# Graph attention with residual LayerNorm: the first edge of each query in blocks of its own, added by VectorE instead of TensorE

## The chip, the cores and the metric

The kernel runs on one core of a Trainium2 chip. The metric is the device time of one execution in microseconds (us). Each kernel was timed on one chip, with the kernel before run beside it in the same rounds. The series of experiments lie on different chips: e1 to e4, and later g1 and g2, on one, f1 to f4 on a second, h1 and h2 on a third. The kernel before took 2595.96 to 2599.37 us on them (medians), so a comparison across series, such as h1 with e2, is good to some 0.3%. All executions that are compared were in the fast state: those of one kernel agree within about half a per cent.

## The reference, cut to what matters

```python
# x: (16, 1024, 512), adj: (1024, 1024) of 0 and 1, the same for all 16 graphs
def _L0_gnn_ref(x, adj, Wq, bq, Wk, bk, Wv, bv, Wo, bo):
    B, N, D, H = (4, 2048, 512, 8); HD = D // H
    b, n, d = x.shape
    q = (x @ Wq + bq).reshape(b, n, H, HD)      # k and v alike
    scores = jnp.einsum('bqhd,bkhd->bhqk', q, k) / jnp.sqrt(jnp.float32(HD))
    scores = scores + (1.0 - adj)[None, None, :, :] * -1000000000.0
    attn = jax.nn.softmax(scores, axis=-1)
    out = jnp.einsum('bhqk,bkhd->bqhd', attn, v).reshape(b, n, d)
    return out @ Wo + bo

x = _layernorm(x + _L0_gnn_ref(x, adj, ...), axis=-1)
```

In these inputs all biases are zero. The adjacency is sparse, so the kernel works on edges and not on the full matrix of scores.

## The kernel before

One "batch" is one of the 16 graphs. Its 1024 queries are eight tiles of 128. The edges of a tile are packed into blocks of 128 edges, one edge to a partition. For each block GpSimd issues two gathers (the q row, and the k and v rows, of each edge). VectorE multiplies q by k and reduces to eight scores, ScalarE takes the exponentials, VectorE weighs v by them (`pv`), and TensorE adds the 128 weighed rows into their queries: a matmul with a matrix of zeros and ones, accumulated in PSUM over the blocks of a tile.

```python
BLOCKS = (11, 6, 4, 4, 3, 3, 3, 3)      # blocks of each tile: 37 a batch
...
def fill_psum(name):                     # all other outputs of TensorE
    return psum.tile([P, HALF], F32, tag="fill", name=name, bufs=4)
...
def add_up(n):
    b, t, i = blocks[n]
    if i == 0:
        SUM[b, t] = psum.tile([P, 2, HALF], F32, tag="sum", name=f"sum_{b}_{t}", bufs=2)
    ...                                                     # two matmuls into it
    if i == BLOCKS[t] - 1:
        later(1, lambda: normalise(b, t))                   # one block later
```

TensorE's other work (the products for q, k and v of the next batch, called "units" here, and the output products `po` of the finished tiles) fills the time between the sums. A loop over the blocks, run when the program is built, deals it out in equal shares, and so fixes the order on every engine:

```python
while n < total or plan or urgent or done or finishing:
    if front_batches < B and front_batches <= max(n // NB, 0) + 1:
        fronts += [...]                  # the next batch's units are let in at block 0
    ...
    elif n % NB == 0:                    # the share of one block, set once a batch
        tiles = len(done) + (NT if n + NB < total else NT + 2)
        share = (sum(u[0] for u in fronts) + tiles * NPAIR * PRODUCT) / NB
    weigh(n + 1); scores(n + 2)
    for fn in plan.pop(n, ()): fn()      # what was put off: normalise, y, ...
    exponentials(n + 2); add_up(n)
    credit += share
    while credit > 0 or urgent:
        ...                              # give out units while there is credit
    credit = min(credit, share)
    n += 1
```

An output tile is finished so: GpSimd adds a bias to the row of x that was loaded for it (`y`), VectorE adds the output product out of PSUM to `y` and takes the statistics, GpSimd makes the scale from them in three small instructions, and ScalarE applies it.

## Time and profile before

| | before |
|---|---|
| time, median of 3 | 2593.45 us (2592.3 to 2593.49) |
| TensorE (PE) busy | 2477.6 us |
| VectorE (DVE) busy | 1968.2 us |
| GpSimd (POOL) busy | 1499.0 us |
| ScalarE (ACT) busy | 698.7 us |
| a steady batch, mean of the fourteen between the first and the last | 153.6 us |

In this table and in those below a batch runs from VectorE's first reduction to scores in it to that in the next. The prediction counts from TensorE's first sum instead; this is why its first batch and last stretch are 147.1 and 135.6 us, and mine 148.9 and 140.3 us.

The busy column of PE is long because ends of matmuls are modelled. The measure that I use below is therefore made from starts: for each matmul the distance to the next start, less the median distance of its kind (0.429 us for a pass of a 512-wide product, 0.222 for a sum, 0.109 for a transpose), summed over a steady batch. I call this sum the **excess** of a batch. It holds both the idle time of TensorE and time at a lower pace, and is good to about 0.1 us. In the kernel before it is 3.16 us, of which 2.07 us are marked idle.

What matters most for this study is the change from one batch to the next. This is the timeline of TensorE there in the kernel before (start, length, instruction; in brackets the idle time before it and what ended it):

```profile
1073.85 0.67 PE L545 MATMUL sum<-pv,sums 128*128 128x256 f32 x2
...
1074.80 3.60 PE L377 MATMUL pq<-wq,xT 128*128 128x512 f32 x8
1078.23 2.74 PE L377 MATMUL pk<-wk,xT 128*128 128x512 f32 x6
1082.85 0.70 PE L545 MATMUL sum<-pv,sums 128*128 128x256 f32 x2 [1.88 <-DVE pv L533]
```

The sum at 1073.85 is block 0 of the new batch, the one at 1082.85 is block 1. Between them TensorE has seven products of the new batch to do, 6.0 us, and then stands for only 1.88 us, although VectorE takes 9.1 us from its weighing of block 0 (1073.02) to that of block 1 (1082.11).

### The profile page before, as it was taken

The numbers are of one execution on the slowest core, as the hardware profiler recorded it, in microseconds if no ns is written. First come the engines' busy times: TensorE is split into PE (matmuls) and PEld (weight loads), VectorE is DVE, ScalarE is ACT, GpSimd is POOL, SyncE is SP. The second block draws the span as 40 slices with busy tenths as digits, with TensorE's granted clock in tenths as the row PEclk, the third lists the DMA queues.
The fourth block names the chain that finished last, engine by engine and source line by source line (L and its number), as shares of the span: only waits on it lengthen the run. The fifth ranks groups of instructions, "written<-read, shape, count | busy, mean of one in ns | idle before, by whom it ended". The sixth has DMA issues, their size and how long they took to land.

```text
span 2594.1 us, 26742 instructions
## 1 busy us (share of the span) xinstructions
PE 2477.6 (96%) x7659; PEld 1352.6 (52%) x7659; DVE 1968.2 (76%) x3613; ACT 698.7 (27%) x1764; POOL 1499.0 (58%) x1717
## 2 busy tenths in 40 slices
PE   6988999999999999999999999999999999999967
PEld 3545555555555555555555555555555555555534
DVE  5668778778778877877777777877877777787766
ACT  1345322222222222222222222222222222222254
POOL 0156755647566574756647465564756557475675
PEclk9989999999999999999999999999999999999978
DMA  4368887887879788787878878787887978878785
GB/s 154 110 243 290 270 291 247 286 270 271 283 237 307 254 291 267 257 292 244 301 253 292 271 235 306 244 294 256 277 288 233 309 251 287 264 256 287 230 277 179
DMA packets 228679, 678.01 MB, mean 261 GB/s; under 512 B 29454, under 2 KB 29466, under 8 KB 228524
## 3 DMA queue, kind: packets, MB, share of 16 engines
q0 software_dynamic: 132608, 465.64, 56.3%
q1 hardware_dynamic: 93344, 205.60, 21.2%
q10 hardware_dynamic: 2572, 4.99, 0.5%
q8 instruction: 62, 1.02, 0.2%
q14 instruction: 93, 0.76, 0.1%
HBM read 541.86 MB, written 134.25 MB: 261 GB/s over the span
## 4 chain that ended last, share of the span: by engine, by line
PE 68%; POOL 11%; DVE 10%; issue 7%; ACT 2%; DMA 1%; ACTq 0%; POOLq 0%; another core or an unknown queue 0%; SPq 0%; DVEq 0%
PE pv L377 16%; PE pk L377 15%; PE pq L377 15%; PE sum L546 7%; PE sum L545 7%; POOL kvg L506 4%; PE po L377 4%; POOL y L461 3%; POOL qg L501 2%; DVE y L468 2%; DVE stats L471 2%; PE pxT L359 2%; PE poT L566 2%; DVE qg L515 1%; DVE pv L533 1%
## 5 line engine op out<-in xcount | busy, mean ns | idle before, releaser
L501 POOL DMA_INDIRECT qg<-q_rows,query_row x592 | 586.9, 991 | 588.1 <-DVE s L517 453.7
L506 POOL DMA_INDIRECT kvg<-kv_rows,key_row x592 | 588.7, 994 | 195.2 <-issue 182.9
L533 DVE TENSOR_TENSOR pv<-kvg,pv 128x512 f32<-128x512 f32 x550 | 394.3, 717 | 223.1 <-ACT pv L522 146.8
L377 PE MATMUL pq<-wq,xT 128*128 128x512 f32 x1024 | 482.7, 597 | 14.7 <-ACT xT L363 13.2
L377 PE MATMUL pk<-wk,xT 128*128 128x512 f32 x1024 | 488.9, 598 | 7.1 <-ACT xT L363 7.1
L377 PE MATMUL pv<-wv,xT 128*128 128x512 f32 x1024 | 479.1, 593 | 0.0
L377 PE MATMUL po<-wo,oT 128*128 128x512 f32 x1024 | 473.9, 602 | 0.0
L515 DVE TENSOR_TENSOR qg<-qg,kvg 128x512 f32<-128x512 f32 x592 | 432.6, 731 | 0.3 <-issue 0.3
L517 DVE TENSOR_REDUCE s<-qg 128x8 f32<-128x512 f32 x592 | 406.1, 686 | 20.5
L545 PE MATMUL sum<-pv,sums 128*128 128x256 f32 x1184 | 361.6, 387 | 46.4 <-DVE pv L533 33.8
L545 PEld LDWEIGHTS sum<-pv,sums 128*128 128x128 f32 x1184 | 222.2, 192 | 326.5 <-issue 239.0
L522 ACT ACTIVATE pv<-s 128x8 f32<-128x8 f32 x592 | 124.1, 210 | 929.2 <-DVE s L517 626.5
L546 PE MATMUL sum<-pv,sums 128*128 128x264 f32 x1184 | 366.6, 392 | 4.6 <-ACT pv L529 2.3
L377 PEld LDWEIGHTS pk<-wk,xT 128*128 128x128 f32 x1024 | 194.3, 192 | 193.3 <-issue 175.7
L377 PEld LDWEIGHTS po<-wo,oT 128*128 128x128 f32 x1024 | 192.9, 194 | 182.6 <-issue 173.3
L377 PEld LDWEIGHTS pv<-wv,xT 128*128 128x128 f32 x1024 | 190.5, 191 | 167.0 <-issue 158.4
L377 PEld LDWEIGHTS pq<-wq,xT 128*128 128x128 f32 x1024 | 187.1, 192 | 159.2 <-issue 135.0
L546 PEld LDWEIGHTS sum<-pv,sums 128*128 128x128 f32 x1184 | 226.2, 192 | 41.6 <-ACT pv L529 6.4
L461 POOL TENSOR_TENSOR y<-y,bo_bc 128x512 f32<-128x512 f32 x128 | 163.4, 1277 | 141.5 <-ACT pv L522 74.7
L468 DVE TENSOR_TENSOR y<-po,y 128x512 f32<-128x512 f32 x128 | 88.0, 688 | 151.5 <-POOL y L461 139.4
L404 DVE TENSOR_TENSOR kv<-pk,bk_bc 128x512 f32<-128x512 f32 x128 | 88.2, 689 | 115.8 <-PE pk L377 87.2
L389 DVE TENSOR_REDUCE nrm<-sq 128x8 f32<-128x512 f32 x256 | 172.9, 676 | 1.4 <-ACT sq L388 1.4
(98 smaller groups left out, 1664.8 us busy)
## 6 DMA issues: line engine op xcount, KB each, us to landing
kv_rows<-kv SPq DMA_DIRECT2D x128, 512.0 KB
x<-in_x_dram SPq DMA_DIRECT2D x128, 256.0 KB
q_rows<-q SPq DMA_DIRECT2D x128, 256.0 KB
y<-in_x_dram SPq DMA_DIRECT2D x128, 256.0 KB
out_dram<-y SPq DMA_DIRECT2D x128, 256.0 KB
qg<-q_rows,query_row POOLq DMA_INDIRECT x592
kvg<-kv_rows,key_row POOLq DMA_INDIRECT x592
a<-in_adj_dram SPq DMA_DIRECT2D x8, 512.0 KB
```

The lines of the kernel that those rows point to most:

```text
L377: nc.tensor.matmul(p, lhs()[:, ts(c, P)], w[:, c, :], start=(c == 0), stop=(c == NPAIR - 1))
L389: later(1, lambda: nc.vector.tensor_reduce(NRM[b][:, i, t, :], sq.rearrange("p (h d) -> p h d", d=HD), axis=AX.X, op=OP.add))
L461: later(2, lambda: nc.gpsimd.tensor_tensor(Y[b, t], Y[b, t], bo_bc, op=OP.add))
L468: nc.vector.tensor_tensor(y, p, y, op=OP.add)
L501: nc.gpsimd.indirect_dma_start(out=QG[n], out_offset=None, in_=q_rows[b % 2], in_offset=bass.IndirectOffsetOnAxis(ap=query_row[:, g:g + 1] ...
L506: nc.gpsimd.indirect_dma_start(out=KG[n], out_offset=None, in_=kv_rows[b % 2], in_offset=bass.IndirectOffsetOnAxis(ap=key_row[:, g:g + 1], ...
L515: nc.vector.tensor_tensor(m, m, KG[n][:, 0:D], op=OP.mult)
L517: nc.vector.tensor_reduce(S[n], m.rearrange("p (h d) -> p h d", d=HD), axis=AX.X, op=OP.add)
L522: nc.scalar.activation(PV[n][:, D:], S.pop(n), AF.Exp)
L533: nc.vector.tensor_tensor(pv[:, 0:D].rearrange("p (h d) -> p h d", d=HD), v[:, D:].rearrange("p (h d) -> p h d", d=HD), pv[:, D:, None].to ...
L545: nc.tensor.matmul(SUM[b, t][:, 0, 0:HD2], m, pv[:, 0:HD2], **kw)
L546: nc.tensor.matmul(SUM[b, t][:, 1, 0:HD2 + HEADS], m, pv[:, HD2:], **kw)
```

## The change

Each query's first edge goes into a block of its own per tile, with edge number p in partition p. Such a block needs no matrix to sort its rows, so VectorE can add it to the tile's sums directly. A batch still has 37 blocks, but TensorE sums only 29. The first-edge block is the last block of its tile. Its q rows are the tile's rows in order, so a plain load replaces the gather. The sums take one PSUM buffer instead of two, and the two banks that come free go to the other outputs, six instead of four.

```diff
-BLOCKS = (11, 6, 4, 4, 3, 3, 3, 3)
+BLOCKS = (10, 5, 3, 3, 2, 2, 2, 2)
+SUM = 0.87
...
-            return psum.tile([P, HALF], F32, tag="fill", name=name, bufs=4)
+            return psum.tile([P, HALF], F32, tag="fill", name=name, bufs=6)
... (the packing of edges leaves out each query's first one)
-                SUM[b, t] = psum.tile([P, 2, HALF], F32, tag="sum", name=f"sum_{b}_{t}", bufs=2)
+                PSUM[b, t] = psum.tile([P, 2, HALF], F32, tag="sum", name=f"sum_{b}_{t}", bufs=1)
...
-            if i == BLOCKS[t] - 1:
-                later(1, lambda: normalise(b, t))
...
+            nc.vector.tensor_tensor(r, s[:, 1, HD2:HD2 + HEADS], pv[:, D:], op=OP.add)
+            nc.vector.tensor_tensor(
+                o.rearrange("p (a d) -> p a d", a=2), s[:, :, 0:HD2], pv[:, 0:D].rearrange("p (a d) -> p a d", a=2),
+                op=OP.add,
+            )
             nc.vector.reciprocal(r, r)
... (one 512-wide product by r instead of two of half the width)
-                    share = (sum(u[0] for u in fronts) + tiles * NPAIR * PRODUCT) / NB
+                    share = (sum(u[0] for u in fronts) + tiles * NPAIR * PRODUCT + NS * SUM) / NB
...
+                if 0 <= n < total and blocks[n][2] == BLOCKS[blocks[n][1]]:
+                    normalise(n)
                 for fn in plan.pop(n, ()):
                     fn()
                 if 0 <= n + 2 < total:
                     exponentials(n + 2)
-                if 0 <= n < total:
+                credit += share
+                if 0 <= n < total and blocks[n][2] < BLOCKS[blocks[n][1]]:
                     add_up(n)
+                    credit -= SUM
...
-                credit += share
```

## The prediction

> **What bounds the kernel now.** I read the page's first two parts first: is one engine full, and for how much of the span?
>
> ```profile
> span 2594.1 us, 26742 instructions
> PE 2477.6 (96%) x7659; PEld 1352.6 (52%) x7659; DVE 1968.2 (76%) x3613; ACT 698.7 (27%) x1764; POOL 1499.0 (58%) x1717
> ...
> PE   6988999999999999999999999999999999999967
> ```
>
> TensorE is full from the second slice to the second last. VectorE is next with 76%. But a busy PE need not be a PE at its pace, so I read the order of time inside one block of edges (TensorE alone; start, length, instruction):
>
> ```profile
> 1001.64 0.59 PE L545 MATMUL sum<-pv,sums 128*128 128x256 f32 x2
> 1002.07 0.61 PE L546 MATMUL sum<-pv,sums 128*128 128x264 f32 x2
> 1002.52 3.60 PE L377 MATMUL pv<-wv,xT 128*128 128x512 f32 x8
> 1005.95 0.59 PE L545 MATMUL sum<-pv,sums 128*128 128x256 f32 x2
> ```
>
> No "idle before" mark stands anywhere. The cost of a thing is the distance between starts, not the length shown: one block's sum takes 1002.52 - 1001.64 = 0.88 us, and four 512-wide products (eight passes) take 1005.95 - 1002.52 = 3.43 us, 0.86 us each. Over the whole trace the median distances give 0.216 + 0.216 + 0.223 + 0.222 = 0.877 us for a block's sum. A batch of the steady part has 128 products, 37 sums, 16 groups of four transposes (0.44 us) and one mean (0.86 us): 109.8 + 32.4 + 7.0 + 0.9 = 150.1 us. Measured from the first sum of one batch to that of the next it takes 153.3 to 154.5 us, of which PE covers about 151.3. So over fourteen sixteenths of the kernel the time is PE's work plus some 2 us a batch. The waits of TensorE say where those are:
>
> ```profile
> PE sum L545 <- DVE pv L533: 33.8, 21, 2.4
> PE pq L377 <- ACT xT L363: 13.2, 1, 13.2
> PE poT L566 <- DVE o L557: 11.2, 13, 5.6
> ```
>
> The first is 1.9 us once at each change of batch: there PE has run out of units and VectorE is late. In time, VectorE alone:
>
> ```profile
> 1080.37 0.69 DVE L468 TENSOR_TENSOR y<-po,y 128x512 f32<-128x512 f32 x1 [5.34 <-POOL y L461]
> ...
> 1082.11 0.68 DVE L533 TENSOR_TENSOR pv<-kvg,pv 128x512 f32<-128x512 f32 x1
> ```
>
> While output tiles are finished, GpSimd's own round (two gathers of about 1.0 us, the add of 1.27 us, three small ones of 0.95 us together, gaps) repeats every 5.17 us, against 4.3 us of PE, and VectorE waits for it, so its lead of about 6.7 us (median from a block's weighing to its sum) is eaten by the end of the batch. The first batch has 19.8 us and the last stretch, 135.6 us from its first sum, has 42.0 us of PE idle: those two are not PE's.
>
> **What the Trainium skill says.** "Perfetto Trace Analysis", section "Tensor Engine Instruction (MATMUL, LD_WEIGHTS)": the end of a matmul in the trace is estimated from its size, not observed. This trace agrees: passes of 0.59 us start 0.43 us apart, so I cost by starts and not by the busy column (361.6 + 366.6 us over 592 blocks would give 1.23 us a block, 40% too much). "PSUM — Partial Sum Buffer", section "Specifications (TRN2)": eight banks of 2 KiB per partition. A sum tile takes two, so two of them and four fill banks before, one and six after, is all of it both times; the second sum buffer is really gone. "VectorE: DVE Perf Modes", section "The perf-mode tier table (the rule you actually need)": an fp32 tensor_tensor runs at 1x from SBUF or PSUM alike. The trace agrees: 688 ns for y<-po,y out of PSUM, a median of 684 ns for qg<-qg,kvg. "SBUF — State Buffer", section "Who interferes with whom": a VectorE instruction with two SBUF inputs contends with a GpSimd one that reads SBUF. The trace fits: that same product has a mean of 731 ns and a longest of 2156 ns.
>
> **The change, part by part.** *Blocks.* 37 blocks a batch become 29 summed ones and 8 of first edges; the gathers, scores, exponentials and weighings stay at 592. The capacity suffices: counted from the inputs, the fullest tile has 1276 edges beyond the first of each query, for 10 x 128 = 1280 places, so the slow fallback is not taken. *TensorE* loses 16 x 8 = 128 sums: 128 x 0.877 = 112.3 us. 120 of them lie in the first fifteen batches. In the thirteen steady ones and the second, 14 x 8 x 0.877 = 98.2 us, everything counts, since PE is the path there. In the first batch, where PE idles 19.8 of 147.1 us for VectorE and ScalarE, I count half of 7.0 us, 3.5 us. In the last stretch none for PE.
>
> *VectorE.* Before, a tile's end costs 0.157 + 0.203 us and two half products that take 0.76 us together: 1.12 us. After, an 8-wide add (estimate 0.16 us, from the 0.157 us of the like-sized row), a 512-wide add of PSUM and SBUF (0.69 us, from y<-po,y), the reciprocal 0.20 us, and a 512-wide product within SBUF (0.72 us, from pv<-kvg,pv): 1.77 us. That is +0.65 us x 128 = 83 us, 5.2 us a batch: 120 us of 153 become 125 of about 147, 85%. It lies beside PE's work. *GpSimd* loses 128 q gathers of 0.99 us (127 us); SyncE issues them as plain 256 KB loads, seven buffers ahead, as the gathers were. *DMA* moves the same bytes in less time: 261 GB/s becomes about 271. The DMA did not hold VectorE up (0.3 us of idle before all 592 products of q and k), so this is hidden.
>
> *Even steps.* The new share charges the sum to the credit, so a block of first edges gets about one more product. PE's time per step stays even, near 4.0 us.
>
> *The single buffer.* The first sum of a tile now waits until VectorE has added the last tile's sums. In VectorE's order these adds follow the next block's weighing (0.7 us), the scores of the one after (1.4 us) and their own 0.9 us: the sum can start some 2.3 us after the weighing it already waited for. Between the two sums lies the block of first edges, in which PE has about 4 us of other units. I laid this demand on the trace before, asking at each tile's first sum how long before it the next scores had ended, less 1.0 us: it holds by 1.2 to 6.1 us in 99 of 112 steady tiles, and fails by 2.2 us in the first tile of a batch, where PE has no units in between. There sum, adds and next sum form a chain; but VectorE is late there for GpSimd's sake, and what is waited for at the first sum is not waited for at the second (the 1.9 us above). Net I count 0 to 2 us a batch, 1 us, 15 us in all, less 3 us for the gathers that GpSimd no longer issues in that very round (three first-edge blocks among its last nine steps).
>
> *Last stretch.* Eight gathers fewer on GpSimd (8 us of its 88.5), 5 us more on VectorE (85.5), neither full: -2 us, and +0.6 us for the longer last tile.
>
> Sum: -98.2 - 3.5 + 15 - 3 - 2 + 0.6 = -91 us; 2593.5 - 91 = 2502. With six fill banks instead of four I expect nothing, since no listed wait of PE is for a free bank. I round to 2500.
>
> **The rivals.** (1) *The single buffer bites at every tile*: 2.3 us x 128 = 294 us if PE waited the full chain each time, or about 100 us if a third did. This would cancel the gain (2500 to 2700 us). For it: strict order on VectorE, which runs fuller than before. Against it: the leads of 1.2 to 6.1 us measured above, and that the adds stand where the old end of tile stood, for which VectorE hardly waited (1.1 us before rden). (2) *VectorE becomes the bound*: its own 125 us, with 8.7 us of waits for GpSimd's y and 9 us for exponentials a batch (139.4 and 146.8 us over 16), come to 143 us against PE's 147. Near, but part of the waits for exponentials is ScalarE standing behind PE's own outputs. If it came true, perhaps 149 to 151 us a batch: 2530 to 2560 us. (3) *The boundary gets better than I count*, since GpSimd's round shortens: no new waits at all, 2485 us. (4) *The loads of q queue up behind SyncE's waits* (508.4 us of it for y before a store): they have some 24 us of lead (six steps of 4.0), so I give it little; it would show as tens of us.
>
> **Range and chances.** The main term is exact work of the full engine; the doubt is all in how much of it new waits return. 2482 (rival 3) to 2530 (rival 2 at its mild end) should hold it 8 times in 10. Faster by over 2% means below 2541.6: 0.92. Within 2%: 0.07. Slower: 0.01.
>
> **What would show it.** PE's busy time should fall by somewhat more than 112 us (by its inflated column 128 x 1.23 = 157 us, to about 2320), with 928 passes per line of the sums where there were 1184; a steady batch should take 146 to 148 us; VectorE's busy time should rise by about 80 us to 2050; the wait of sum for VectorE's add should be about 15 times 1 to 3 us, at the changes of batch alone. I am wrong in the single-buffer step if that wait appears some 100 times, in the VectorE step if weighed blocks (pv) come late all through a batch, and in the main term if PE's gaps grow without either.

## The result

| | before, same rounds | after |
|---|---|---|
| time, median of 4 | 2593.47 us (2592.3 to 2597.06) | 2680.2 us (2679.08 to 2682.64) |
| ratio | 1 | 1.0333, 95% interval 1.0315 to 1.0351 |
| PE / DVE / POOL busy | 2477.6 / 1968.2 / 1499.0 us | 2386.0 / 2005.0 / 1395.7 us |
| first batch / steady batch / last stretch | 148.9 / 153.6 / 140.3 us | 144.4 / 159.7 / 147.2 us |
| excess of a steady batch | 3.16 us | 16.04 us |

A ratio here and below is the mean time of one kernel's fast runs over that of the kernel before in the same rounds, so it is not quite the ratio of the medians. The kernel became 3.3% slower, where I had predicted 3.6% faster. The page of the changed kernel, in its first two parts:

```profile
span 2680.9 us, 25437 instructions
...
PE 2386.0 (89%) x7123; PEld 1273.8 (48%) x7123; DVE 2005.0 (75%) x3637; ACT 695.5 (26%) x1764; POOL 1395.7 (52%) x1589
PE   7988798998989989798997989899898997989765
PEclk9989899998989989898998989999898998989877
```

TensorE did lose work: 536 matmuls (512 of them passes of the sums) and 91.6 us of its busy time. But its row of full slices now has an 8 or a 7 in every second or third place, and its granted clock (PEclk) dips in the same rhythm. Forty slices and sixteen batches: something happens once a batch. The waits of TensorE give it one name (total, times, longest):

```profile
PE sum L562 <- DVE rden L575: 230.2, 23, 15.3
```

230.2 us is more than twice the whole expected gain, and it is 23 waits, fifteen of them over 13 us (there are fifteen changes of batch), not the 128 that a wait at every tile would give. The timeline of TensorE at the change of batch, to be compared with the one of before above:

```profile
1093.03 0.59 PE L562 MATMUL sum<-pv,sums 128*128 128x256 f32 x2
1093.46 0.61 PE L563 MATMUL sum<-pv,sums 128*128 128x264 f32 x2
1107.80 1.19 PE L562 MATMUL sum<-pv,sums 128*128 128x256 f32 x2 [13.72 <-DVE rden L575]
1108.78 1.09 PE L563 MATMUL sum<-pv,sums 128*128 128x264 f32 x2
1109.66 1.91 PE L385 MATMUL pq<-wq,xT 128*128 128x512 f32 x2
```

The sum at 1093.03 is block 35, the last summed block of the old batch, and the one at 1107.80 is block 0 of the new batch. There is no product between them: TensorE has no product to do in blocks 35 and 36, and stands 13.72 us. The starts after it show a second loss: two sum passes take 0.98 us instead of 0.43, and one product takes 1.71 us (1109.66 to the next start at 1111.37) instead of 0.86. TensorE runs at half its pace for some 5 us after the stall, which costs another 2.5 us here. What VectorE does in these 14 us, in its own timeline:

```profile
1094.14 0.69 DVE L476 TENSOR_TENSOR y<-po,y 128x512 f32<-128x512 f32 x1 [1.43 <-POOL y L469]
...
1103.23 0.69 DVE L476 TENSOR_TENSOR y<-po,y 128x512 f32<-128x512 f32 x1 [5.35 <-POOL y L469]
...
1104.98 0.68 DVE L550 TENSOR_TENSOR pv<-kvg,pv 128x512 f32<-128x512 f32 x1
...
1106.97 0.68 DVE L571 TENSOR_TENSOR o<-sum,pv 128x512 f32<-128x512 f32 x1
1107.57 0.19 DVE L575 RECIPROCAL rden<-rden 128x8 f32<-128x8 f32 x1
```

VectorE finishes two output tiles of the old batch, the first after a wait of 1.43 us for GpSimd and the second after one of 5.35 us. Then it weighs block 0 (1104.98), and then it adds the last tile's sums (1106.97), which frees the single PSUM buffer. The total of its waits for GpSimd's `y` has hardly changed: 139.4 us before, 144.3 us after. The 5.34 us wait was there before the change too, as the prediction shows. It has not grown. It has moved in front of a sum before which TensorE has no work.

### The profile page after: what moved, and what is told of

Read it like the earlier page. It is cut to its first block, busy times and chain, and to the rows that moved or that the text cites. A ratio compares the mean times of both kernels' runs of the same rounds, so it can differ in the third digit from the quotient of the medians.

```text
span 2680.9 us, 25437 instructions
## 1 busy us (share of the span) xinstructions
PE 2386.0 (89%) x7123; PEld 1273.8 (48%) x7123; DVE 2005.0 (75%) x3637; ACT 695.5 (26%) x1764; POOL 1395.7 (52%) x1589
## 4 chain that ended last, share of the span: by engine, by line
PE 57%; POOL 13%; DVE 13%; issue 11%; DMA 5%; ACT 1%; another core or an unknown queue 0%; POOLq 0%; SPq 0%; ACTq 0%; DVEq 0%
PE pq L385 14%; PE pk L385 13%; PE pv L385 12%; PE sum L562 5%; PE sum L563 5%; POOL kvg L519 5%; POOL qg L514 4%; PE po L385 4%; POOL y L469 3%; DVE qg L528 2%; DMA kvg<-kv_rows,key_row 2%; DVE s L530 2%; DVE stats L479 2%; DVE y L476 2%; DVE pv L550 2%
## 5 line engine op out<-in xcount | busy, mean ns | idle before, releaser
L514 POOL DMA_INDIRECT qg<-q_rows,query_row x464 | 466.7, 1006 | 715.7 <-DVE s L530 520.1
L562 PE MATMUL sum<-pv,sums 128*128 128x256 f32 x928 | 295.0, 401 | 253.2 <-DVE rden L575 230.2
L550 DVE TENSOR_TENSOR pv<-kvg,pv 128x512 f32<-128x512 f32 x550 | 383.5, 697 | 172.8 <-ACT pv L539 128.5
L385 PE MATMUL pq<-wq,xT 128*128 128x512 f32 x1024 | 494.9, 614 | 13.2 <-ACT xT L371 13.2
L385 PE MATMUL pk<-wk,xT 128*128 128x512 f32 x1024 | 476.0, 593 | 0.0
L385 PE MATMUL po<-wo,oT 128*128 128x512 f32 x1024 | 462.9, 599 | 0.0
L528 DVE TENSOR_TENSOR qg<-qg,kvg 128x512 f32<-128x512 f32 x592 | 415.4, 702 | 0.0
L562 PEld LDWEIGHTS sum<-pv,sums 128*128 128x128 f32 x928 | 177.6, 198 | 464.8 <-issue 408.3
L563 PE MATMUL sum<-pv,sums 128*128 128x264 f32 x928 | 297.5, 404 | 0.8 <-ACT pv L546 0.8
L385 PEld LDWEIGHTS pq<-wq,xT 128*128 128x128 f32 x1024 | 194.2, 199 | 172.7 <-issue 150.8
L476 DVE TENSOR_TENSOR y<-po,y 128x512 f32<-128x512 f32 x128 | 87.9, 687 | 164.4 <-POOL y L469 144.3
L563 PEld LDWEIGHTS sum<-pv,sums 128*128 128x128 f32 x928 | 183.7, 199 | 31.6 <-ACT pv L546 3.6
```

Of the source, the lines that this page charges most:

```text
L385: nc.tensor.matmul(p, lhs()[:, ts(c, P)], w[:, c, :], start=(c == 0), stop=(c == NPAIR - 1))
L476: nc.vector.tensor_tensor(y, p, y, op=OP.add)
L514: nc.gpsimd.indirect_dma_start(out=QG[n], out_offset=None, in_=q_rows[b % 2], in_offset=bass.IndirectOffsetOnAxis(ap=query_row[:, g:g + 1] ...
L528: nc.vector.tensor_tensor(m, m, KG[n][:, 0:D], op=OP.mult)
L550: nc.vector.tensor_tensor(pv[:, 0:D].rearrange("p (h d) -> p h d", d=HD), v[:, D:].rearrange("p (h d) -> p h d", d=HD), pv[:, D:, None].to ...
L562: nc.tensor.matmul(PSUM[b, t][:, 0, 0:HD2], m, pv[:, 0:HD2], **kw)
```

## The experiments

Twelve kernels ran; all gave correct results. The names used: theory A, the single PSUM buffer is to blame; B, VectorE's longer work; C, neither of them, but the plain loads of q or the lower clock by itself. After the first four runs I added D, the dealing out of units. The units of the last blocks of a batch, as the build-time loop gives them out (worked out by running its bookkeeping alone; it agrees with the traces at the places that I checked). SUM is a block's sum, `po4 x4` four products of output tile 4, oT a transposed tile:

```text
block    before            after             after, units 3 blocks early
33       SUM po3 x3        po4 x3            po3 x4
34       SUM po4 x4        SUM oT po5 x4     SUM pq oT pq x3
35       SUM oT po5 x4     SUM               SUM pk x3
36       SUM               (nothing)         pk pv x4
0        SUM pq x4 pk x3   SUM pq oT pq x3 pk x4   SUM xT oT pq x2
```

All results in one table. Excess and period are the means over the fourteen steady batches of the profiled run.

| run | median us | ratio to before [95%] | period us | excess us |
|---|---|---|---|---|
| before | 2593 to 2599 | 1 | 153.6 | 3.16 |
| after | 2680.20 | 1.0333 [1.0315, 1.0351] | 159.7 | 16.04 |
| e1, two sum buffers | 2653.86 | 1.0218 [1.0200, 1.0236] | 157.4 | 13.91 |
| e2, units let in early | 2497.48 | 0.9618 [0.9600, 0.9635] | 146.6 | 3.22 |
| e3, before with one sum buffer | 2815.28 | 1.0833 [1.0812, 1.0855] | 168.0 | 17.49 |
| e4, four fill banks | 2684.64 | 1.0336 [1.0314, 1.0358] | 159.7 | 16.25 |
| f1, count mended | 2581.83 | 0.9937 [0.9921, 0.9954] | 153.0 | 9.59 |
| f2, count and carry mended | 2510.00 | 0.9664 [0.9648, 0.9681] | 147.5 | 4.34 |
| f3, no add on GpSimd | 2527.48 | 0.9731 [0.9715, 0.9747] | 150.0 | 6.56 |
| f4, before with early units | 2544.44 | 0.9799 [0.9782, 0.9815] | 149.8 | -0.07 |
| g1, e2 with two sum buffers | 2542.55 | 0.9784 [0.9756, 0.9812] | 149.7 | 6.36 |
| g2, f2 with two sum buffers | 2508.03 | 0.9655 [0.9636, 0.9673] | 147.2 | 4.23 |
| h1, e2 with four fill banks | 2521.46 | 0.9712 [0.9696, 0.9728] | 148.5 | 5.09 |
| h2, e2 with the adds first | 2489.26 | 0.9586 [0.9567, 0.9605] | 146.3 | 2.90 |

Period less excess is TensorE's bare work. It is 149.8 to 150.5 us in the three kernels without the change (before, e3, f4), and 143.0 to 143.7 us in all the others. The change takes some 7 us from a batch everywhere; the rows differ in the excess.

### e1: two sum buffers again

```diff
-   fill ... bufs=6        +   fill ... bufs=4
-   sum  ... bufs=1        +   sum  ... bufs=2
```

> The changed kernel with two buffers for the sums again and four fill banks, nothing else. Theory A (the single buffer makes the first sum of each batch wait, while TensorE has no other work): the 13 us stall at each of the 15 changes of batch goes, waits of sum for the add (rden) fall from 230 us to under 15 us, and the time is what the removed sums are worth: 2485 to 2510 us. Rival B (VectorE has too much to do in the changed kernel, 2005 us busy): the stall comes back as a wait of sum for pv, 2560 us or more. Rival C (the plain loads of q on SyncE or the lower clock by itself): still about 2680 us.

Measured: 2653.86 us (2651.31 to 2656.67), against 2680.20. The wait changes its name and not much else:

```profile
PE sum L562 <- DVE pv L550: 177.3, 19, 12.8
```

Now the first sum waits for the weighing of its own block, 11.1 to 12.8 us at each change of batch. In the timeline of VectorE above that weighing stands 2 us before the adds. So the single buffer was only the last 2 us of each stall, and theory A falls as the main cause: 26 us of the 180 between the measured 2680 and my 2500. Theory B had forecast this very wait, so e1 alone leaves B standing; e2 decides about it.

### e2: the next batch's units three blocks early

```diff
-   front_batches <= max(n // NB, 0) + 1
+   front_batches <= max((n + 3) // NB, 0) + 1
```

> The changed kernel with its single sum buffer, but the products of the next batch may start 3 blocks before that batch instead of at its first block. Theory A: TensorE gets about 7 us of units in the two last blocks of a batch, where it had none, so each stall falls from 13 to some 6 us, and the clock sags less: 2680 - 15 x 7 - 15 x 2 = about 2545 us (2500 to 2580). If the lack of units has nothing to do with it (the wait for the add being as long wherever the units lie): within 1% of 2680 us. Rival B (VectorE full): within 2% of 2680 us as well, as VectorE's work is the same.

Measured: 2497.48 us (2495.68 to 2501.99), lower than even A allowed. No PSUM buffer was added, VectorE's busy time even rises to 2035.0 us, 67 us over before, and the plain loads of q stay: neither the buffer nor theories B and C explain the stall. But this run doesn't show that the want of units alone does, since the new order also takes away most of VectorE's waits for GpSimd's `y`, 144.3 us in after:

```profile
DVE y L476 <- POOL y L469: 19.7, 9, 4.5
```

Both halves of the stall went at once; f2 and f3 below take them one by one. The edit also sets the share lower, 3.752 us a block instead of 3.845 (by the same bookkeeping; f1 explains the difference). What is left stands at an ordinary end of a tile (waits of TensorE, then its timeline there):

```profile
PE sum L562 <- DVE rden L575: 63.0, 37, 7.8
```

```profile
1011.83 6.17 PE L385 MATMUL po<-wo,oT 128*128 128x512 f32 x14
1019.54 0.67 PE L562 MATMUL sum<-pv,sums 128*128 128x256 f32 x2 [1.55 <-DVE rden L575]
```

Seven products lie before that sum, and VectorE is still 1.55 us later. This is the wait for the single buffer that the prediction had looked for; it costs some 2.4 us of idle time a batch.

### e3: the kernel before with one sum buffer

```diff
-   fill ... bufs=4        +   fill ... bufs=6        (the kernel before)
-   sum  ... bufs=2        +   sum  ... bufs=1
```

> The kernel before with one sum buffer and six fill banks; first edges stay in the summed blocks. Theory A: the single buffer alone makes the stall. In the kernel before VectorE adds nothing but normalises after the second block of the next batch has been weighed, at about 11.7 us after the last sum of a batch, where 1.9 us was lost: some 10 us and 2 us of clock more at each of 15 changes, 2593 + 15 x 12 = about 2770 us (2720 to 2800). If the first-edge blocks and VectorE's adds are the cause (rival B): within 1% of 2593 us.

Measured: 2815.28 us (2809.75 to 2817.67), 8.3% slower than before and worse than any theory said.

```profile
PE sum L545 <- DVE o L557: 241.9, 66, 13.7
```

```profile
1162.17 1.19 PE L545 MATMUL sum<-pv,sums 128*128 128x256 f32 x2 [9.30 <-DVE o L557]
```

In the old order the end of a tile comes one block after the tile's last sum, so with one buffer the next tile's first sum waits for it at several tiles (1.33, 1.33 and 1.93 us in most batches) and, at the change of batch, behind VectorE's wait for GpSimd (9.3 us). So one buffer cost 218 us in that order (2815.28 against 2597.24 for before in these rounds) and 26 us in the changed one (e1 against after). The price of a single buffer depends on where its reader stands in VectorE's order; the changed kernel needed its new place for the adds to afford it.

### e4: four fill banks

```diff
-   fill ... bufs=6        +   fill ... bufs=4
```

> The changed kernel with one sum buffer and only four fill banks (two banks left unused). No listed wait of TensorE, before or after, is for a fill bank, so the two banks gained should be worth nothing: within 0.5% of 2680 us. If six fill banks let TensorE run ahead and hide part of the stall: 2700 us or more.

Measured: 2684.64 us (2681.26 to 2690.52), 0.2% over after, as expected. With this schedule the two extra banks are worth nothing. This also makes e1 a clean test, since e1 had to give them up.

### f1 and f2: mending the count

Why has TensorE no units in block 35? The share of a block is set at block 0 from `len(done) + 8` tiles. In the kernel before, no tile is in `done` at that moment. In the changed one, a tile is normalised in the step of its last block instead of one later, and the old batch's tile 6 is already in `done`: it is counted beside the eight tiles of the new batch, although one of the new batch's tiles will likewise be left over at the next change. In microseconds, the units of the next batch are 8 x (12 x 0.86 + 0.44) = 86.08, a tile's output products are 4 x 0.86 = 3.44 and the sums 29 x 0.87 = 25.23. The share is (86.08 + 9 x 3.44 + 25.23) / 37 = 3.845 us instead of (86.08 + 8 x 3.44 + 25.23) / 37 = 3.752 us. Over 37 blocks this is 3.44 us too much, so the units are used up nearly one block early. The credit left from the last batch takes them another part of a block forward.

```diff
-   tiles = len(done) + (NT if n + NB < total else NT + 2)
+   tiles = (NT if n + NB < total else NT + 2)
+   credit = min(credit, 0.0)          # this line in f2 alone
```

> Theory D (formed after the first four runs: the sums' single buffer is worth some 2 us of each 13 us stall; the rest is that TensorE has no unit left in the last two blocks of a batch, of which the last has no sum either, so it stands before the next batch's first sum two blocks early, while VectorE goes through two rounds of y at GpSimd's pace). One cause of that: in the changed kernel a tile is done one block sooner, so tile 6 of the last batch is already counted as done when the share is set and counted again among the eight to come; the share is 3.84 where 3.75 would do. This run drops the double count, nothing else. Replaying the schedule gives four products of po in the last but one block, where there were none, and still none in the last. Theory D: the stall falls from 13 to 3 to 8 us, 2680 - 15 x (5 to 10) - 15 x 1 to 2 = 2500 to 2590 us. Theory A (the single buffer): no change, over 2660 us.

> The count mended as in f1, and unused credit not carried into the next batch: by the replay four products of po come to lie in the very last block of a batch and TensorE has units in every block, without any unit of the next batch being let in early. Theory D: as good as the early units, 2485 to 2520 us. If instead it was the early start of the next batch's loads and products that helped in the early-units run: clearly above, over 2560 us.

Measured: f1 2581.83 us (2579.9 to 2583.92), f2 2510.00 us (2507.86 to 2512.39). The first line takes the wait of the sums for VectorE from 230.2 to 122.0 us, both lines take it to 72.3 us (f1, then f2; the third line is VectorE's own wait in f2):

```profile
PE sum L562 <- DVE rden L575: 122.0, 21, 13.2
PE sum L562 <- DVE rden L575: 72.3, 23, 13.0
DVE y L476 <- POOL y L469: 101.3, 56, 7.7
```

VectorE keeps 101.3 of its 144.3 us of waits for `y` here, so f2 is a cleaner test of the units than e2. Theory D holds: two lines of build-time arithmetic, which change no computing instruction but only the order, are worth 170 us. With the units still let in at block 0, this is the change as I had predicted it, and it is 10 us off my 2500.

### f3: GpSimd's add taken away

```diff
-   later(2, lambda: nc.gpsimd.tensor_tensor(Y[b, t], Y[b, t], bo_bc, op=OP.add))
```

The result stays right only because the bias is zero in these inputs.

> The changed kernel without GpSimd's add of the output bias to y (correct for these inputs alone, where that bias is zero); units and sum buffer as changed. Theory D: VectorE's waits for y at the end of a batch (144 us in all, 1.4 and 5.4 us of each 13.7 us stall) go, and the stall falls to 6 to 7 us: 2680 - 15 x 7 - 15 x 1 = about 2560 us (2520 to 2600). If GpSimd's round is not what VectorE is waiting for behind these adds, it stays within 1% of 2680 us.

Measured: 2527.48 us (2526.7 to 2528.64). The schedule of the units is that of after, and the stall at the change of batch shrinks from 13.72 to 4.25 us:

```profile
1051.99 1.19 PE L561 MATMUL sum<-pv,sums 128*128 128x256 f32 x2 [4.25 <-DVE rden L574]
```

With nothing of GpSimd's to wait for there, VectorE's delay before the adds shrinks, and 9.5 us of each stall go with it. So the stall has two causes that must meet: TensorE without units, and VectorE held by GpSimd. To remove either one mends most of it (f2 and f3). They are not independent: the order of the units also sets how long VectorE waits, as e2 shows. The last stretch also falls, from 147.2 to 128.0 us.

### f4: the control, early units in the kernel before

```diff
-   front_batches <= max(n // NB, 0) + 1             (the kernel before)
+   front_batches <= max((n + 3) // NB, 0) + 1
```

> The kernel before, with units of the next batch let in 3 blocks early as in e2: the control. It loses only 2 us of TensorE at each change of batch, so at most 15 x 2 = 30 us are to be had: 2560 to 2590 us. Then 65 to 90 us of e2's gain belong to the first-edge blocks themselves, against the 105 us that the removed sums are worth. If e2's gain were all from the early units, this would be near 2500 us too.

Measured: 2544.44 us (2543.18 to 2547.85), more than I had expected. The excess of a steady batch goes to zero: TensorE runs through without a gap. So much of e2's gain belongs to the early units and not to the change. With early units in both, the change is worth 0.9618 / 0.9799 = 0.9815, or 1.9%: of the 6.4 us a batch that TensorE no longer does here (period less excess: 149.8 against 143.4), 3.3 come back as excess (3.22 against -0.07).

### g1, g2 and h1: two sum buffers in the mended kernels

```diff
-   fill ... bufs=6        +   fill ... bufs=4        (g1: in e2; g2: in f2; h1: in e2, this line alone)
-   sum  ... bufs=1        +   sum  ... bufs=2        (g1 and g2)
```

> First-edge blocks, units let in 3 blocks early (e2) and two sum buffers with four fill banks (e1) together. The steady batch of e2 takes 146.7 us with 2.6 us of waits for the adds and some 1.5 us of lower clock after them; without them it should take 149.8 (f4's batch, which has no idle TensorE) - 7.0 (eight sums) = 142.7 us. So 2497 - 14 x 4 = about 2441 us (2430 to 2465), and against f4 about 100 us: the removed sums at their full price. If VectorE's longer end of tile is a limit after all, waits for pv take the place of those for the adds and the time stays at 2485 us or more.

> The mended share (f2) with two sum buffers. If the single buffer costs some 2.5 us a batch once TensorE has units everywhere: 2510 - 14 x 2.5 to 4 = 2455 to 2475 us. If the wait moves to pv (as it did in e1): within 0.5% of 2510 us.

> e2 (one sum buffer, early units) with four fill banks instead of six, two banks unused. It asks why g1 (two sum buffers, four fill banks) took 2543 us and not 2441. If the fill banks are what g1 lacked (its trace shows TensorE waiting 2.2 us a batch for ScalarE's copy of v out of a bank before a product of q): this has the same waits and takes 2520 to 2560 us. If two sum buffers by themselves do harm: it stays at 2497 us, within 0.5%.

Measured: g1 2542.55 us (2538.13 to 2549.07), 45 us slower than e2 where I had expected a gain of 56. g2 2508.03 us (2506.39 to 2509.3), the same as f2: the wait moved from the adds to the weighing, as its expectation allowed. h1 2521.46 us (2517.33 to 2523.96). The waits of TensorE, one line from g2, two from g1 and one from h1:

```profile
PE sum L562 <- DVE pv L550: 38.6, 31, 12.8
PE pq L385 <- ACT kv L418: 30.2, 12, 7.1
PE poT L582 <- DVE o L577: 29.0, 39, 1.5
PE pq L385 <- ACT kv L418: 27.1, 13, 8.1
```

The wait for `kv` is one for a free fill bank: ScalarE must first copy another product out of it. h1, which has one sum buffer and four fill banks, shows 27.1 us of it too, and e2 with six banks shows none. So 24 of the 45 us are the two fill banks: e4's "worth nothing" held only while TensorE stood still for another reason. The other 21 us (19 by the ratios, as g1 and h1 ran on different chips) come with the second sum buffer, and most of them are time at a lower pace. g2 gave up the same two banks, and four banks alone in f2 were not run, so its second sum buffer is not priced by itself. The idle time of a steady batch is the same in g1 and h1 (4.00 and 3.92 us), but the excess is 1.3 us larger in g1. There, the wait for a bank is 2.18 us long, comes 0.6 us after the end of a wait of 0.85 us for `o`, and is followed, at once or a few passes later, by passes about twice the usual distance apart. In h1 the two waits are 1.56 and 1.59 us long and 17 us apart, and the passes after them keep their pace. Why the two waits lie so close in g1, I did not settle.

### h2: the adds ahead of the weighing

```diff
+   if 0 <= n < total and blocks[n][2] == BLOCKS[blocks[n][1]]:
+       normalise(n)                    # moved up to here, in e2
    if 0 <= n + 1 < total:
        weigh(n + 1)
    ...
-   if 0 <= n < total and blocks[n][2] == BLOCKS[blocks[n][1]]:
-       normalise(n)
```

> e2 with VectorE's adds of a tile placed before the weighing and scores of their block instead of after. e2 still loses 2.6 us a batch (three waits of 0.4 to 1.6 us for these adds) and some 1.5 us of lower clock. If they come from the adds standing behind 2.1 us of other VectorE work, all go: 2497 - 14 x 2.6 to 4 = 2440 to 2465 us. If VectorE then waits for TensorE's last sum instead and loses its lead: 2497 us or more.

Measured: 2489.26 us (2482.68 to 2491.01). This has the lowest ratio of the study, 4.1% faster than before, but its interval overlaps that of e2, so the adds' new place is not shown to gain anything, and it misses what I expected. The wait for the single buffer did vanish; TensorE's sum waits for the weighing instead, because VectorE now stands still itself:

```profile
PE sum L562 <- DVE pv L550: 45.0, 19, 5.3
DVE rden L570 <- PE sum L563: 111.2, 75, 3.7
```

VectorE reaches the adds before TensorE has made the last sum of the tile, waits, and is late for the weighing behind it. The chain of last sum, adds, weighing and next sum stays closed whichever of VectorE's two parts goes first. In every second steady batch the remaining 2.08 us wait was also followed by half pace.

## Why the prediction was wrong

**The work removed: right.** 928 passes per line of the sums stand in the trace, as predicted, and TensorE's bare work of a batch fell from 150.4 to 143.6 us, 6.8 us where I had counted 7.0. The busy column fell by 91.6 us (117.9 in e2), not by the 157 that I had named as a sign: the eight costliest lines of TensorE on the page before add to 2812 us, more than its busy time of 2477.6, since passes overlap, so a line's column can't be taken off the total. The first batch gained 4.5 us, where I had counted 3.5.

**VectorE's added work: right for the parts, too high for the total.** The four instructions at a tile's end have means of 158, 681, 193 and 746 ns, 1.78 us, against 1.77 predicted. The busy time rose by 36.8 us in after and 67 us in e2, not by 83: in after the products of q and k became shorter on average (731 to 702 ns) and the weighings too (717 to 697 ns), 28 us together. VectorE did not become the bound (rival 2), and the loads of q held up nothing (rival 4): the products of q and k have no idle time before them in after.

**The single buffer at every tile (rival 1): wrong as a mechanism.** There are 23 waits, not some 100. I had the place right (the fifteen changes of batch) and the size wrong: 13 to 15 us each, not 1 to 3.

**"Even steps": the step that failed.** I wrote that "PE's time per step stays even, near 4.0 us". I had read this from the code of the share and not from the order of the built program. The order of both programs was there to be read: it shows blocks 35 and 36 without units. The change counts the left-over tile twice and has it ready one block sooner, so TensorE runs dry a block earlier, and the last block of a batch no longer has even a sum. f1 and f2 show it: 98 and 170 us.

**"What is waited for at the first sum is not waited for at the second": the other half of it.** I knew the 5.34 us wait of VectorE for GpSimd and charged it once, as the 1.9 us that TensorE already lost. In the kernel before, block 0's sum and seven products hid all but 1.88 us of the 9.1 us between VectorE's two weighings. In the changed kernel the same delay falls before block 0's first sum, where nothing hides it. So the term "0 to 2 us a batch, 1 us" measured 11.4 us more of idle time (13.46 against 2.07) and 1.5 us more of lower pace. f3 shows that 9.5 of the 13.7 us go with GpSimd's add, and e1 that the buffer itself is 2 us.

**The sum.** Fourteen batches at +6.08 us, -4.5 us in the first batch and +6.9 us in the last stretch are +87.5 us, against 86.7 measured. The last stretch, for which I had -1.4 us, I didn't take apart; f3 shows that GpSimd's add weighs in it.

**"With six fill banks instead of four I expect nothing": right for the changed kernel (e4), wrong in general.** With the schedule mended they are worth 24 us (h1 against e2).

That f2 came to 2510 and e2 to 2497, near the predicted 2500, should not be read as more than it is. f2 is the fair test: its steady batch of 147.5 us lies in the 146 to 148 that I had named, so the working fits apart from the order of units. e2 gains from early units what the single buffer takes back.

## What to carry to other kernels

When a change removes work from the full engine of a statically dealt schedule, look up in the built order what stands in its place at each seam, above all where the next batch's work is let in; a counter that is read one step earlier can move all the filling work. A wait on a side engine costs what the full engine lacks in work at that moment, so a delay of VectorE with the same 5.3 us wait in it cost 1.9 us in one place and 13.7 us in another. Test an extra buffer again after the main stall is mended, since its worth can turn from nothing to one per cent, or change sign.

## What the Trainium skill lacked or had wrong

- "TensorE: Matmul & The Clock Gate", section "Part 1: The HAM clock gate (the "warmup" mystery)", says that the array falls to half its clock after an idle window of about 3.4 us. Half pace after the long stalls agrees: all fifteen of 13 us and more in after, and all fifteen of 11 us and more in e1, were followed by passes at about twice the usual distance, at a cost of 1.5 to 3.1 us each. But 3.4 us is no safe limit from below: waits of 1.88 to 1.90 us in the kernel before were followed by half pace 3 times in 13, those of 2.08 us in h2 5 times in 10. Nor does a longer wait always slow the very next passes: after five of the thirteen waits of 4.25 to 4.6 us in f3 the half pace began only two to four passes later, and cost 1.8 us instead of 2.3 to 2.6. None of the waits of 1.55 to 1.60 us in e2 and h1 was followed by it.
- "Perfetto Trace Analysis", section "Optimization Strategy", says that a gap which repeats on the engine that should be full can mean that too little SBUF or PSUM is there for the next tile. Here such a gap of 13.7 us a batch even named the reader of the single PSUM buffer, and a second buffer took only 2 us of it (e1); what lacked was other work to issue (f2), while VectorE waited for GpSimd (f3). The section doesn't name this case.
- "PSUM — Partial Sum Buffer" gives the banks but not what a second accumulator is worth in a schedule like this one. Here going without it cost 218 us in one order of VectorE's work (e3) and 26 us in another (e1); with the count mended a second one, bought with two fill banks, changed nothing (2 us, g2 against f2), and with early units having it cost about 20 us (g1 against h1).
